# A four-layer graph network on one core: score banks seeded by VectorE, bias banks by ScalarE, and ScalarE's tile operand left in its own bank

## The chip, the core and the metric

The kernel runs on one NeuronCore of a Trainium2 chip. Four engines compute: TensorE (PE, matmuls, writes only PSUM), VectorE (DVE), ScalarE (ACT) and GpSimd (POOL, which works on SBUF alone here); SyncE (SP) issues transfers. PSUM has eight banks of 128 partitions x 512 fp32 values. The metric is device microseconds of one execution; lower is better. Three runs of the kernel before gave 4797.05 to 4799.08 us, median 4798.81.

## What is computed

Input `x` has 64 batches of 256 nodes with 128 features; `adj` is 256 x 256. Four layers, each on a layer norm with ReLU of what the layer before gave, and each added to its input:

```
layer 0: 5 gated steps   m = adj @ h; z, r = sigmoid(...); hv = tanh(...); h = (1-z)*h + z*hv
layer 1: relu([h, adj^T h, (2 adj^T adj^T - 1) h, ...] @ Theta1 + bias)
layer 2: y = (adj @ h + h) @ weight + bias;  y / max(|y|, 1e-12)
layer 3: e[i,j] = sum_f a[f] * leaky(s1[i,f] + s2[j,f] + b_lin[f]) + adj[i,j]
         out = sigmoid(softmax_j(e) @ h)
```

Layer 3 is most of the work: for each batch 256 x 256 node pairs times 256 features f, with a nonlinear step for each, so nothing but the sum over f can be a matmul.

## The kernel before

Batches are taken in 32 pairs. A **front** (`front`, L485) does layers 0 to 2 and layer 3's projections for one pair, as a chain of some 109 steps; the first pair is done as two single batches (`alone`), whose code paths differ a little. All tensors of a step are 128 x 512 (features x 2 batches x 256 nodes, or nodes x features), one bank.

Layer 3 is done in **slots**, 64 for a pair, 32 for each of its two **units**. A unit covers 128 rows i for both batches of the pair. A slot treats 4 rows x 2 batches; it needs two **tiles** of 128 x 2048, one for each half k of the 256 features. A tile holds min(s2, row of s1) or the ReLU that stands for it. Any of three engines can make a tile (`work_on_tile`, L908):

- VectorE, k = 0: one TENSOR_TENSOR (L928) that reads `s1a` in SBUF and `s2a` in the bank where TensorE wrote it.
- ScalarE, k = 1: 8 ACTIVATEs of 128 x 256 (L940), which read a bank and take a column of `s1b` as bias.
- GpSimd, k = 0 or 1: 8 TENSOR_SCALARs of 128 x 256 (L945) on copies in SBUF, `s2c` and `s2n`.

The operand that ScalarE reads comes about in three moves: TensorE projects it into a bank, ScalarE copies it to SBUF (`s2n`, L763), the bank is given back, and at the first ScalarE tile of a pair ScalarE copies `s2n` into one bank kept for this alone all along (`S2P`, L935).

`score` (L989) sums a tile over features: four matmuls side by side, each against a window of a column of signs, into the unit's **score bank**. A unit's first score begins the bank: TensorE multiplies the adjacency by an identity into it (8 matmuls of 128 x 256, through `side_by_side`, L403), and every score accumulates on that. For 600 of the 2048 slots the two tiles are added first by a DMA that GpSimd issues (L965), so one score serves for both. In all 3496 scores.

When a unit's 64 tiles are in, its **tail** (`tail`, L803) follows: VectorE adds `lin` (a row vector that a DMA has spread over the partitions, `rows`, L753) to the bank (L809), adds the part of one odd feature (L814), takes the maximum (L819); ScalarE exponentiates; TensorE transposes and multiplies; then the division, tanh and output.

In layers 1 and 2 of a front, `project_token` (L436) multiplies into a bank `po`, and VectorE adds the bias there, bank to bank (L664, L687), before it goes on (L668; L691 on ScalarE).

**The order** of every engine's instructions is fixed when the program is built, by a planner in the kernel (from L1032 on). It keeps a clock per engine with a cost for each step (`ran`, L107; a tile 2.2 on VectorE, 2 x 1.43 on ScalarE, 4 x 0.9 on GpSimd; a score 0.86). On the engine whose clock is lowest it takes, of the steps that are ready, a tail's first, then a front's, then a score, then a new tile. A result is seen by others `SEEN` later (0.18 us for ScalarE), and for ScalarE a further `behind` later, which grows by 0.024 of its work and shrinks by its gaps:

```python
        if engine == ACT:
            behind[0] = max(0.0, behind[0] - (start - clock[ACT])) + 0.024 * us
        clock[engine] = start + us
        return clock[engine] + SEEN[engine] + (behind[0] if engine == ACT else 0.0)
```

Fronts are held to due times by the number of scores done, and may not run more than two steps ahead. Tiles have 14 buffers, banks are in a list `spare` with the time when each comes free (`take`, L121, gives the earliest), and at most two score banks are open. Each engine then runs its fixed list in order, and waits at each instruction for what it needs.

Of the kernel before, what the change touches and what calls it, by code (L numbers as in the profile page):

```python
# [9 lines left out]
AF = mybir.ActivationFunctionType  # L10
# [4 lines left out]
P = 128  # L15
# [17 lines left out]
def kernel(  # L33
# [70 lines left out]
    SEEN = {PE: 0.25, DVE: 0.14, ACT: 0.18, POOL: 0.13}  # L104
    behind = [0.0]

    def ran(engine, us, *after):  # L107
        start = max(clock[engine], 0.0, *after)
        if engine == ACT:
            behind[0] = max(0.0, behind[0] - (start - clock[ACT])) + 0.024 * us  # L110
        clock[engine] = start + us
        return clock[engine] + SEEN[engine] + (behind[0] if engine == ACT else 0.0)

# [6 lines left out]

    def take():  # L121

        spare.sort(key=lambda b: b[1])
        return spare.pop(0)

# [282 lines left out]
    def project(pp, w, t, start=True, stop=True):  # L408

        side_by_side(pp[:, 0:t.shape[1] * N], w, flat(t), start, stop)  # L410

    def mix_nodes(pm, h, a):

        nb = h.shape[1]
        pm = by_feature(pm, nb)
        for b in range(nb):
            for c in range(NC):
                side_by_side(pm[:, b, :], h[:, b, c, :], a[:, c, :], c == 0, c == NC - 1)

# [15 lines left out]

    def project_token(pp, pairs):  # L436

        nb = pairs[0][0].shape[1]
        pp = by_token(pp, nb)
        for b in range(nb):  # L440
            for c in range(NC):
                for k, (t, w) in enumerate(pairs):
                    side_by_side(pp[:, b, c, :], t[:, b, c * P:(c + 1) * P], w, k == 0, k == len(pairs) - 1)

# [36 lines left out]
    READY = {}  # L481
    S2P = []
    OF_FIRST = {}

    def front(p, batches):  # L485
# [164 lines left out]
        yield ACT, t  # L650
        hT, t = copied("hT", b, t, bufs=4)
        yield PE, t_h, 1
        b = take()
# [3 lines left out]
        c2T, t = copied("c2T", b, t)  # L657
        yield PE, t, 1
        po = take()
        project_token(po[0], [(hT, th[:, 0, :]), (c1T, th[:, 1, :]), (c2T, th[:, 2, :])])  # L660
        t = ran(PE, PRODUCTS[nb], t, po[1])
        yield DVE, t
        pt = rows_of(turned_of(po))
        nc.vector.tensor_add(pt, pt, bias1.unsqueeze(1).to_broadcast([P, nb * NC, D]))  # L664
        t = ran(DVE, ELEMENTS[nb], t)
        yield DVE, t
        x2 = token("x2", tag="x12", bufs=3)
# [5 lines left out]
        h = token("h")  # L673
        t = yield from norm(x2, t, h)
        yield PE, t, 1
        b = take()
# [3 lines left out]
        yT, t = copied("yT", b, t)  # L680
        yield PE, t, 1
        po = take()
        project_token(po[0], [(yT, w2)])
        t = ran(PE, PRODUCT[nb], t, po[1])
        yield DVE, t
        pt = rows_of(turned_of(po))
        nc.vector.tensor_add(pt, pt, bias2.unsqueeze(1).to_broadcast([P, nb * NC, D]))  # L687
        t = ran(DVE, ELEMENTS[nb], t)
        yield ACT, t
# [67 lines left out]
        yield PE, t_hT, 1  # L757
        b = take()
        project(b[0], w2n[:, P:2 * P], hT)
        t = ran(PE, PROJECT[nb], t_hT, b[1])  # L760
        yield ACT, t
        s2n = kept("s2n", [N])
        nc.scalar.copy(s2n, seen(b))  # L763
        t_2 = ran(ACT, COPY[nb], t)
        spare.append([b[0], t_2])
        s2p = []
        if alone:
            yield ACT, t_2, not S2P
            if not S2P:
                S2P.append(take())  # L770
            s2p.append(by_feature(S2P[0][0])[:, own])
            nc.scalar.copy(s2p[0], s2n)
            ran(ACT, COPY[nb], t_2, S2P[0][1])
        yield PE, t_hT, 1
# [16 lines left out]
        spare.append([b[0], t_n])  # L791
        ops = dict(x3=x3, h3=h3, s1=(s1a, s1b), s2a=seen(s2a), bank=s2a, s2c=s2c, s2n=s2n, s1o=s1o, s2o=s2o, s2p=s2p,
                   lin=lin, t_lin=t_lin, since=(max(t_n, t_s2a), max(t_b, t_2), max(t_b, t_2)), alone=alone,
                   left=SLOTS // 2 if alone else SLOTS)
        for u in batches:
            READY[p, u] = ops
        tiles.extend([t, max(t_b, t_n, t_lin)] for t, _ in lent)

# [4 lines left out]
    def tail(u, pe, since):  # L803

        ops = READY[u]
        x3, h3, pe, lin = ops["x3"], ops["h3"], [by_feature(pe[0])[:, k, :] for k in range(NB)], ops["lin"]
        yield DVE, max(since, ops["t_lin"])
        used = banks_of.pop(u)
        nc.vector.tensor_add(by_feature(used), by_feature(used), lin.to_broadcast([P, NB, N]) if ops["alone"] else lin)  # L809
        t = ran(DVE, ELEMENTS[2], since, ops["t_lin"])  # L810
        yield DVE, t
        sc = feat("sc", **SHORT)
        for k, (b, c) in enumerate(across(u)):
            nc.vector.scalar_tensor_tensor(sc[:, k, :], ops["s2o"][:, b, :], ops["s1o"][:, b, c:c + 1], pe[k], op0=OP.min, op1=OP.add)  # L814
        t = ran(DVE, 0.8, t)
        spare.append([used, t])
# [91 lines left out]
    def work_on_tile(e):  # L908
        if e not in begun:
            k = part_of(e)  # L910
            tiles.sort(key=lambda t: t[1])
            begun[e] = [slot(k), k, *tiles.pop(0), 0]
            following[k] += 1
            held[e] += 1
            if k == 0:
                READY[where(begun[e][0])[0]]["left"] -= 1
        n, k, t, free, part = begun[e]
# [8 lines left out]
        if e == DVE:  # L926
            whole = [P, 4, NB, N]
            nc.vector.tensor_tensor(t, rows.to_broadcast(whole), ops["s2a"].unsqueeze(1).to_broadcast(whole), op=OP.min)  # L928
            done = ran(DVE, 2.2, since)
            ops["bank"][1] = max(ops["bank"][1], done)  # L930
            parts = 1
        elif e == ACT:
            if not ops["s2p"]:
                ops["s2p"].append(by_feature(S2P[0][0]))
                nc.scalar.copy(ops["s2p"][0], ops["s2n"])  # L935
                ran(ACT, 0.62, since)
            parts = 2
            for g in (2 * part, 2 * part + 1):
                for b in range(NB):
                    nc.scalar.activation(t[:, g, b, :], other(ops["s2p"][0], b), AF.Relu, bias=rows[:, g, b], scale=-1.0)  # L940
            done = ran(ACT, 1.43, since)
        else:
            parts = 4
            for b in range(NB):
                nc.gpsimd.tensor_scalar(t[:, part, b, :], other(ops["s2n" if k else "s2c"], b), rows[:, part, b],  # L945
                                        MOST_NEGATIVE, op0=OP.min, op1=OP.max)
            done = ran(POOL, 0.9, since)
        begun[e][4] += 1
        if part + 1 == parts:
# [3 lines left out]
            else:  # L953
                made.append((done, n, k, t, e))
        if k == 0 and not ops["left"] and ops["bank"][0] is not None:
            spare.append(list(ops["bank"]))
            ops["bank"][0] = None

# [4 lines left out]
    def add_pair(n):  # L963
# [7 lines left out]
        made.append((done, n, 2, t, None))  # L971

    def score_ready():

        best = None
        for tile_ in made:
            u, _ = where(tile_[1])
            since = tile_[0]
            if u not in left:
                if len(banks_of) == 2 or not spare:  # L980
                    continue
                since = max(since, min(b[1] for b in spare))
            if best is None or since < best[0]:
                best = since, tile_
        return best
# [3 lines left out]
    def score(tile_):  # L989
        since, n, k, t, e = tile_  # L990
        u, r = where(n)
        made.remove(tile_)
        if u not in left:
            left[u] = 64
            bank, free = take()
            banks_of[u] = bank
            for x, (_, c) in enumerate(across(u)):
                side_by_side(by_feature(bank)[:, x, :], ident, adj_n[:, c, :], x == 0, False)
            ran(PE, 0.87, since, free)
        left[u] -= 2 if k == 2 else 1  # L1000
        pe = banks_of[u]
        w = win if e == ACT else win_n
# [29 lines left out]
    def chain_ready(key, e):  # L1032

        engine, since, bank, gate = (*CHAINS[key][1], 0, None)[:4] if len(CHAINS[key][1]) < 4 else CHAINS[key][1]
        if engine != e or bank and not spare or gate and not gate():
            return None
        if not isinstance(key, tuple) and 1 <= key < NPAIR and spare:

            due = STEPS_OF_FRONT * (scored[0] / (2 * SLOTS) - (key - 2)) / SPREAD
            if CHAINS[key][2] > due + AHEAD:  # L1040
                return None
        return max(since, min(b[1] for b in spare)) if bank else since

# [14 lines left out]
    while scored[0] < 2 * NSLOT or CHAINS:  # L1058
# [12 lines left out]
        else:  # L1071
            since = tile_ready(e)
            if since is not None:
                todo.append((since, (3,), None))
            pair = pair_ready()
            if e == POOL and pair and e not in begun:
                todo.append((pair[0] + SLACK, (2,), pair[1]))
        ready = [x for x in todo if x[0] <= now[e] + 0.05]
        if ready:
# [5 lines left out]
            elif e == PE:  # L1085
                score(what)
            elif rank == 2:
                add_pair(what)
# [38 lines left out]
```

## Time and profile before

| | us |
|---|---|
| median of three runs | 4798.81 |
| the profiled execution | 4796.37 |
| its span | 4794.6 |
| TensorE busy, matmuls | 4744.3 |
| VectorE, ScalarE, GpSimd busy | 4651.6, 4608.6, 4636.5 |
| VectorE tiles, L928, x1747 | 3909.3 |
| ScalarE tiles, L940, x9976 | 3937.4 |
| GpSimd tiles, L945, x6408 and x2408 | 3056.0, 1167.1 |
| scores, L1004, x27968 (two matmul records each) | 2241.6 and 1317.3 |

A line of the groups reads: source line, engine, operation, what it writes and reads, shapes and count; then the busy time of the group, the mean duration of one, and how long its engine had been idle before it. A duration on ScalarE or VectorE includes the landing of its result, which overlaps with the next instruction: 9976 activations of 704 ns on average would be 7023 us, and their busy time is 3937. So the time that an instruction takes from a full engine is read from the distance of two starts. The clock granted to TensorE was 0.999 of full speed. The first 148 us are set-up and the first pair's front, in which VectorE, ScalarE and GpSimd are not yet full; from 4540 us on no fronts are left.

### The profile page before, as it was taken

What the parts mean: (1) busy time and instruction counts of PE and PEld (TensorE: products, weight loads), DVE (VectorE), ACT (ScalarE), POOL (GpSimd) and SP (SyncE); (2) the same over time, 40 slices, a digit from 0 to 9 for tenths busy, and PEclk for the clock granted to TensorE, in tenths of its full rate; (3) what the DMA queues carried; (4) which work ended last, traced back from release to release, by engine and by line L of the source; (5) the groups of instructions that cost most, each with busy time, mean ns of one, the idle gap of its engine ahead of it and who ended that gap; (6) DMA issues with size and microseconds to landing.
All of it is one profiled execution on the core that took longest, in us unless ns stands there. A gap on an engine that the chain in (4) does not pass through costs nothing.

```text
span 4794.6 us, 134766 instructions
## 1 busy us (share of the span) xinstructions
PE 4744.3 (99%) x52583; PEld 1758.2 (37%) x52583; DVE 4651.6 (97%) x3568; ACT 4608.6 (96%) x12063; POOL 4636.5 (97%) x9919
## 2 busy tenths in 40 slices
PE   9999999999999999999999999999999999999999
PEld 4333333433333333333333333333333333333333
DVE  6999999999999999999999999999999999999999
ACT  6999999999999999999999999999999999999999
POOL 3999999999999999999999999999999999999998
PEclk9999999999999999999999999999999999999999
DMA  1767777777676777777777777777767777777730
GB/s 39 151 142 154 150 146 150 145 145 158 141 157 143 143 155 152 151 146 145 149 152 149 147 150 146 151 155 146 148 138 158 150 151 151 148 150 143 151 66 5
DMA packets 131529, 672.82 MB, mean 140 GB/s; under 512 B 14920, under 2 KB 50120, under 8 KB 54088
## 3 DMA queue, kind: packets, MB, share of 16 engines
q0 software_dynamic: 86400, 629.18, 65.6%
q1 hardware_dynamic: 43768, 35.01, 2.5%
q8 instruction: 411, 6.73, 0.6%
q14 instruction: 230, 1.88, 0.1%
q10 hardware_dynamic: 720, 0.00, 0.0%
HBM read 26.48 MB, written 8.52 MB: 7 GB/s over the span
## 4 chain that ended last, share of the span: by engine, by line
PE 69%; DVE 10%; POOL 8%; DMA 6%; ACT 5%; issue 2%; POOLq 0%; SPq 0%; DVEq 0%; ACTq 0%
PE bank L1004 43%; PE bank L403 23%; DVE rl L928 8%; POOL rl L945 7%; DMA rl<-rl 5%; ACT rl L940 3%; PE bank L434 2%; PE bank L426 1%; POOL rl L965 1%; ACT h L478 0%; DVE bank L613 0%; DVE d L609 0%; DVE hT L617 0%; DVE rh L574 0%; POOL mv L398 0%
## 5 line engine op out<-in xcount | busy, mean ns | idle before, releaser
L940 ACT ACTIVATE rl<-bank,s1b 128x256 f32<-128x256 f32 x9976 | 3937.4, 704 | 47.5 <-DMA rl<-rl 18.7
L928 DVE TENSOR_TENSOR rl<-s1a,bank 128x2048 f32<-128x2048 f32 x1747 | 3909.3, 2276 | 41.4 <-DMA rl<-rl 19.5
L945 POOL TENSOR_SCALAR rl<-s2n,s1b 128x256 f32<-128x256 f32 x6408 | 3056.0, 799 | 19.5 <-ACT s1b L780 5.1
L1004 PE MATMUL bank<-rl,win_n 128*32 128x512 f32 x17992 | 2241.6, 593 | 20.8 <-DMA rl<-rl 14.9
L1004 PE MATMUL bank<-rl,win 128*32 128x512 f32 x9976 | 1317.3, 593 | 0.0
L945 POOL TENSOR_SCALAR rl<-s2c,s1a 128x256 f32<-128x256 f32 x2408 | 1167.1, 763 | 3.5
L1004 PEld LDWEIGHTS bank<-rl,win_n 128*32 128x32 f32 x17992 | 577.4, 110 | 1197.8 <-issue 978.2
L965 POOL DMA_DIRECT2D rl<-rl x600 | 644.9, 1090 | 3.6 <-PE bank L1004 0.9
L1004 PEld LDWEIGHTS bank<-rl,win 128*32 128x32 f32 x9976 | 324.8, 110 | 636.4 <-issue 516.5
L403 PE MATMUL bank<-mT,wts 128*32 128x512 f32 x2480 | 328.1, 592 | 0.5 <-ACT mT L526 0.5
L403 PE MATMUL bank<-adj_t,h 128*32 128x256 f32 x4960 | 296.8, 379 | 3.8 <-ACT h L628 3.8
L403 PEld LDWEIGHTS bank<-adj_t,h 128*32 128x32 f32 x4960 | 160.0, 110 | 160.8 <-issue 49.6
L478 ACT ACTIVATE h<-x,mv 128x128 f32<-128x128 f32 x376 | 163.8, 584 | 26.8 <-POOL mv L474 26.5
L403 PE MATMUL bank<-mT,w 128*32 128x512 f32 x1240 | 165.3, 593 | 0.6 <-ACT bank L570 0.5
L570 ACT ACTIVATE bank<-bank,gate_b 128x512 f32<-128x512 f32 (+1 forms) x165 | 137.6, 834 | 29.4 <-PE bank L403 16.5
L403 PE MATMUL bank<-rh,u5t 128*32 128x512 f32 x1240 | 164.9, 592 | 0.0
L403 PE MATMUL bank<-hT,wts 128*32 128x512 f32 x1240 | 163.5, 593 | 0.0
L403 PEld LDWEIGHTS bank<-mT,wts 128*32 128x32 f32 x2480 | 82.3, 110 | 185.1 <-issue 149.4
L398 POOL TENSOR_TENSOR mv<-mv,minus_half 128x4 f32<-128x4 f32 (+1 forms) x132 | 133.8, 1014 | 11.0
L593 ACT ACTIVATE bank<-bank,gate_b 128x512 f32<-128x512 f32 (+1 forms) x165 | 134.6, 816 | 10.2 <-PE bank L403 10.1
L526 ACT COPY mT<-bank 128x512 f32<-128x512 f32 x155 | 123.8, 799 | 19.6 <-PE bank L403 19.6
L606 ACT ACTIVATE bank<-bank,gate_b 128x512 f32<-128x512 f32 x155 | 128.8, 831 | 6.3 <-PE bank L403 6.3
(206 smaller groups left out, 3274.2 us busy)
## 6 DMA issues: line engine op xcount, KB each, us to landing
rl<-rl POOLq DMA_DIRECT2D x600, 1024.0 KB, 8.3
rows<-row SPq DMA_DIRECT2D x31, 512.0 KB
xin<-in_x_dram SPq DMA_DIRECT2D x64, 128.0 KB
out_dram<-o SPq DMA_DIRECT2D x64, 128.0 KB
row<-quarter SPq DMA_DIRECT2D x62, 2.0 KB
rows<-row SPq DMA_DIRECT2D x2, 256.0 KB
w_raw<-in_L_gnn_w_w_dram SPq DMA_DIRECT2D x3, 128.0 KB
rl<-in_L_gnn_Theta_dram SPq DMA_DIRECT2D x1, 320.0 KB
```

The lines of the kernel that those rows point to most:

```text
L398: nc.gpsimd.tensor_tensor(t, t, minus_half[:, 0:t.shape[1]], op=OP.pow)
L403: nc.tensor.matmul(o[g:g + 32], w[:, g:g + 32], t, start=start, stop=stop, skip_group_check=True)
L478: nc.scalar.activation(h[:, k, :], s[:, k, :], AF.Relu, bias=mv[:, k, 0:1], scale=mv[:, k, 1:2])
L526: nc.scalar.copy(c, seen(bank))
L570: nc.scalar.activation(seen(r), seen(pr), AF.Tanh, bias=br, scale=0.5)
L593: nc.scalar.activation(seen(pr), seen(pr), AF.Tanh, bias=bz, scale=0.5)
L606: nc.scalar.activation(seen(pv), seen(pv), AF.Tanh, bias=bh_n, scale=-1.0)
L928: nc.vector.tensor_tensor(t, rows.to_broadcast(whole), ops["s2a"].unsqueeze(1).to_broadcast(whole), op=OP.min)
L940: nc.scalar.activation(t[:, g, b, :], other(ops["s2p"][0], b), AF.Relu, bias=rows[:, g, b], scale=-1.0)
L945: nc.gpsimd.tensor_scalar(t[:, part, b, :], other(ops["s2n" if k else "s2c"], b), rows[:, part, b], MOST_NEGATIVE, op0=OP.min, op1=OP.max)
L965: nc.gpsimd.dma_start(out=t.rearrange("p g b n -> p (g b n)"), in_=z.rearrange("p g b n -> p (g b n)"), accum_op=OP.add)
L1004: nc.tensor.matmul(pe[g * 32:(g + 1) * 32, :], w[:, 31 - r:63 - r], flat(t[:, g]), start=False, stop=(left[u] == 0), skip_group_check=True)
```

## The change

- **Score banks.** For all units but the first pair's two, VectorE writes the sum of the adjacency and `lin` into the score bank ahead of the unit's first score (`fill_bank`, L1006 of the changed file), when the pair's operands are ready and one engine's next tile lies in that unit. TensorE's copy through the identity goes, and so does VectorE's addition of `lin` in the tail. The scores accumulate on what VectorE wrote.
- **Biases.** ScalarE copies the bias into the bank `po` ahead of the product, and the product accumulates on it; VectorE's additions (L664, L687) go. The bank is taken one mixing step earlier.
- **Which banks.** [...] a set `WRITTEN` keeps account of banks that matmuls have wholly written, and only those may be filled by VectorE or ScalarE (`take(2)`). `mix_nodes` and `project_token` start fresh once per bank instead of once per piece, so that the whole bank stays marked.
- **ScalarE's operand.** It reads the bank into which TensorE projected it. That bank is given back when the pair's last ScalarE tile has begun. The private bank and its 31 copies (and 2 halves) go.
- **The planner** loses `behind`: a ScalarE result is seen 0.18 us after its step in every case. `take` prefers, of the banks that are free by now, those not in `WRITTEN`.

```diff
-    behind = [0.0]
     def ran(engine, us, *after):
         start = max(clock[engine], 0.0, *after)
-        if engine == ACT:
-            behind[0] = max(0.0, behind[0] - (start - clock[ACT])) + 0.024 * us
         clock[engine] = start + us
-        return clock[engine] + SEEN[engine] + (behind[0] if engine == ACT else 0.0)
+        return clock[engine] + SEEN[engine]
...
+    WRITTEN = set()
+    def of_spare(bank):
+        return [b for b in spare if bank < 2 or id(b[0]) in WRITTEN]
-    def take():
-        spare.sort(key=lambda b: b[1])
-        return spare.pop(0)
+    def take(bank=1):
+        b = min(of_spare(bank), key=lambda b: (max(b[1], min(now.values())), bank < 2 and id(b[0]) in WRITTEN, b[1]))
+        spare.remove(b)
+        if bank < 2:
+            WRITTEN.discard(id(b[0]))
+        return b
...
+        if not alone:
+            yield ACT, t, 2
+            po = take(2)
+            nc.scalar.copy(rows_of(turned_of(po)), bias1.unsqueeze(1).to_broadcast([P, nb * NC, D]))
+            t_po = ran(ACT, COPY[nb], po[1])
         yield PE, t_h, 1
         b = take()
         mix_nodes(b[0], h, adj_2)
...
-        project_token(po[0], [(hT, th[:, 0, :]), (c1T, th[:, 1, :]), (c2T, th[:, 2, :])])
+        project_token(po[0], [(hT, th[:, 0, :]), (c1T, th[:, 1, :]), (c2T, th[:, 2, :])], fresh=alone)
...
-        nc.vector.tensor_add(pt, pt, bias1.unsqueeze(1).to_broadcast([P, nb * NC, D]))
+        if alone:
+            nc.vector.tensor_add(pt, pt, bias1.unsqueeze(1).to_broadcast([P, nb * NC, D]))
...
-        nc.vector.tensor_add(by_feature(used), by_feature(used), lin.to_broadcast([P, NB, N]) if ops["alone"] else lin)
+        if ops["alone"]:
+            nc.vector.tensor_add(by_feature(used), by_feature(used), ops["lin"].to_broadcast([P, NB, N]))
...
-            if not ops["s2p"]:
-                ops["s2p"].append(by_feature(S2P[0][0]))
-                nc.scalar.copy(ops["s2p"][0], ops["s2n"])
-                ran(ACT, 0.62, since)
-                    nc.scalar.activation(t[:, g, b, :], other(ops["s2p"][0], b), AF.Relu, bias=rows[:, g, b], scale=-1.0)
+                    nc.scalar.activation(t[:, g, b, :], other(ops["s2b"], b), AF.Relu, bias=rows[:, g, b], scale=-1.0)
...
+    def bank_ready():
+        u = next((u for u in UNITS if u not in left and u not in banks_of), None)
+        if u not in READY or READY[u]["alone"] or len(banks_of) == 2 or all(where(slot(k))[0] < u for k in range(3)):
+            return None
+        return (max(READY[u]["t_lin"], min(b[1] for b in of_spare(2))), u) if of_spare(2) else None
+    def fill_bank(u):
+        bank, free = take(2)
+        nc.vector.tensor_add(by_feature(bank), adj_n[:, u[1]:u[1] + 1, :].to_broadcast([P, NB, N]), READY[u]["lin"])
+        banks_of[u] = bank, ran(DVE, ELEMENTS[2], free, READY[u]["t_lin"])
```

Layer 2's bias is treated as layer 1's is. On VectorE the fill stands in the planner's choice after tails' and fronts' steps and ahead of new tiles.

## The prediction

> **What bounds the kernel now.** I read the page's busy shares first, then the table by stage, the chain, the groups of the lines that change, and stretches of each engine's timeline. The page's opening lines:
>
> ```profile
> span 4794.6 us, 134766 instructions
> PE 4744.3 (99%) x52583; PEld 1758.2 (37%) x52583; DVE 4651.6 (97%) x3568; ACT 4608.6 (96%) x12063; POOL 4636.5 (97%) x9919
> ...
> PE 69%; DVE 10%; POOL 8%; DMA 6%; ACT 5%; issue 2%; POOLq 0%; SPq 0%; DVEq 0%; ACTq 0%
> ```
>
> All four engines are nearly full; the last line, the chain that ended last, is on TensorE for 69% of its length, so no other engine can be called the bound alone. By stage, the part without start and end (148 to 4540 us):
>
> ```profile
> core 0: us, PE busy (x) PEld busy (x) DVE busy (x) ACT busy (x) POOL busy (x), PEclk, DMA share, GB/s
> ...
> 2100.00:2800.00 700.00, 696.29 (x7644) 251.62 (x7640) 687.82 (x515) 679.94 (x1782) 690.49 (x1473) 1.00 0.73 148
> ...
> sum 4392.00, PE 4364.79 PEld 1605.74 DVE 4309.21 ACT 4263.65 POOL 4336.88; mean PE 623.54 PEld 229.39 DVE 615.60 ACT 609.09 POOL 619.55
> ```
>
> Idle in those 4392 us: TensorE 27, VectorE 83, ScalarE 128, GpSimd 55. ScalarE alone has room worth naming. A tile goes to whichever engine the planner finds free, so an engine's share of tiles follows from its other work.
>
> Busy times of groups overlap; what an engine gives per instruction when full is read from starts in its timeline:
>
> ```profile
> 1327.96 6.36 ACT L940 ACTIVATE rl<-bank,s1b 128x256 f32<-128x256 f32 x16
> 1333.67 1.13 ACT L526 COPY mT<-bank 128x512 f32<-128x512 f32 x1
> ```
>
> 16 activations in 1333.67 − 1327.96 = 5.71 us: 0.357 each, 2.86 per tile of 8.
>
> ```profile
> 831.43 0.59 ACT L935 COPY bank<-s2n 128x512 f32<-128x512 f32 x1
> 832.06 3.03 ACT L940 ACTIVATE rl<-bank,s1b 128x256 f32<-128x256 f32 x8
> ```
>
> A ScalarE copy from SBUF into a bank: 0.63.
>
> ```profile
> 1119.00 0.69 DVE L613 SCALAR_TENSOR_TENSOR bank<-bank,d 128x512 f32<-128x512 f32 x1
> 1119.60 2.27 DVE L928 TENSOR_TENSOR rl<-s1a,bank 128x2048 f32<-128x2048 f32 x1
> 1121.80 0.68 DVE L617 SCALAR_TENSOR_TENSOR hT<-bank,hT 128x512 f32<-128x512 f32 x1
> ```
>
> VectorE: 0.60 for 512 columns, 2.20 for a tile.
>
> ```profile
> 835.94 1.05 PE L403 MATMUL bank<-adj_n,ident 128*32 128x256 f32 x16
> 836.80 1.04 PE L1004 MATMUL bank<-rl,win 128*32 128x512 f32 x8
> ```
>
> TensorE: 0.86 for one unit's copy of the adjacency. In the chain, 24 GpSimd instructions of L945 take 10.92 us: 0.455 each, 3.64 per tile of 8.
>
> **The change, part by part.** Counts are from the instruction orders of the two built programs.
>
> TensorE. 62 of 64 adjacency copies go: 62 × 0.86 = −53 us. No matmul is added: the bias steps only turn a fresh start into accumulation. Scores stay 3496.
>
> VectorE. 62 adds of biases (L664, L687, 0.69 a row, 0.60 in sequence) go: −37. The 62 adds of `lin` in the tails go and 62 fills with the adjacency plus `lin` come: alike in size, taken at nothing. VectorE also gets 4 tiles fewer (1747 to 1743): −9. Sum −46.
>
> The fill is the one operation with no row of its kind: both inputs lie in SBUF, while L809, which it replaces, and the tiles (L928) read one from PSUM. By the row (L633 reads SBUF and a bank in 0.68, L809 in 0.69) it costs its 0.60 and nobody else anything. The Trainium skill speaks against it (SBUF — State Buffer, "Who interferes with whom"): a VectorE instruction with two SBUF inputs takes its second through the read port that GpSimd uses, and whichever of the two starts second stands until the first is done. GpSimd reads SBUF all the time (0.455 per instruction). By the rule GpSimd stands up to 62 × 0.60 = 37 us and VectorE, arriving mid-instruction, 62 × 0.23 = 14. No row here shows it. Bounds: 0 and 37 + 14; a gain is excluded, since the columns are the same. I take it as it says, about 37 and 14 of engine time.
>
> ScalarE. 31 copies into the private bank (0.63) go, −20; 62 bias copies come at the same row, +39 (bounds 0.47, the PSUM-to-SBUF copy at 1333.67 to 1334.14, and 0.63: +29 to +39). Tiles go from 1247 to 1264: 17 × 2.86 = +49. Sum +68, against 128 us idle.
>
> GpSimd. Tiles 1102 to 1089: 13 × 3.64 = −47. The 600 adding DMAs stay, as do SP's issues; no queue gets a transfer more.
>
> Banks. The private bank is freed, but each pair keeps a second bank until its last ScalarE tile has begun, so where two pairs meet four banks are held (three before); a score bank is filled some 4 VectorE tiles ahead, and a bias bank is taken before the mixing matmuls instead of after. Only banks that matmuls have wholly written may serve. The price is a front held up for want of a bank. In the order, the operands of a pair stand about 7.5 ScalarE tiles before their first use, before and after alike, so I take nothing; the bound is one bank's turnover, about 1 us in each of 31 pairs, hidden under 7.5 × 2.86 = 21 us of lead.
>
> New waits. The fill waits for the DMA of `rows`; queued behind it are VectorE's tiles. It stands about 11 tiles (24 us) behind the transpose that starts those rows, and in the trace the rows are issued 4 us after that transpose: nothing. The product with theta waits for ScalarE's bias copy, which is issued ahead of a mixing step (1.7 us of matmuls) and an evacuation: hidden, about 0.6 us per use on a front that is early anyway. What this cover hides costs 62 × 0.6 = 37 us of front, not of span.
>
> The planner's lag term. `behind` goes: in the plan a ScalarE result is now visible 0.18 us after its slot always. The rows show why the term was there: an L940 lasts 449 ns at least, 659 in the median, 704 on average, 1930 at most, so results land 0.255 us later on average than a fresh one, more after long runs without a gap. ScalarE's gaps shrink from 128 to about 60, so runs get longer. The LDWEIGHTS waits put down to an L940 are 603 (79.6, 83.5, 25.6 and 14.3 us by line), 0.34 each, where the ordinary spacing is 0.29: the handoff is just in time. If a third of these are late by 0.25, TensorE loses 50; VectorE takes about 400 ScalarE results in its fronts and loses perhaps 10. Bounds: below nothing is excluded, since an optimistic plan makes nothing land sooner; above, 603 × 0.255 = 154.
>
> **The sum.** In engine time: TensorE −53 + 50 = −3; VectorE −46 + 14 + 10 = −22; GpSimd −47 + 37 = −10; ScalarE +68 into its gaps. Without lag and port it would be −53, −46, −47. TensorE's late starts do not add to the lock, and the 14 tile buffers let an engine catch up, so I put the losses on the span at half of what they cost the engine: −46 (VectorE and GpSimd agree) + about 12 for the port (half of 14 and 37 averaged) + about 10 to 15 for the lag = −22 to −24. The profiled execution took 4796.4 (span 4794.6 and 1.8 around it), 2.4 under the median of the runs, 4798.8. So 4798.8 − 24 = 4775.
>
> **The rivals.**
> A. Nothing lost: port and lag cost nothing and the plan's relief comes through. 4799 − 46 = 4753. For it: three engines get the same relief. Against: two of the costs have reasons. With forecast and A in one family, chance of the forecast's case (4753 to 4789) 0.45, of A or better 0.08.
> B. No gain: only the engines that make tiles bind. Then TensorE's 53 us are cover. VectorE's 37 us are worth 37 / 2.2 = 17 tiles, ScalarE's 19 extra cost 7, GpSimd's 37 of blocking cost 10: zero tiles, 4799. For it: GpSimd hardly waits (8 us in the steady part). Against: the orders give VectorE and GpSimd 46 and 47 us less work, so the plan has found the time. 0.16.
> C. Slower: ScalarE's late results. Place: the first LDWEIGHTS behind an L940 or a front's evacuation. If all 603 just-in-time handoffs stand by half the lag, 603 × 0.13 = 78: 4799 − 46 + 78 = 4831. It decides from 46 / 603 = 0.076 us per handoff on. For it: the term was cut while ScalarE is given 68 us more. Against: PE's own idle is 27 us in all, and most waits fall into its queue's spacing. 0.31.
> D. The change not doing what it says: a fill that isn't accumulated on; the bookkeeping of written banks answers that, and it would move no time.
>
> **How the numbers follow.** 4775 is the likeliest case. A measurement of this kernel tells about 0.2% from no change, so faster is below 4789.2 and slower above 4808.4: 0.53, 0.16, 0.31. The likeliest case alone reaches from 4753 to 4789; for 8 in 10 the range goes from 4745 (A with a little of ScalarE's gaps) into C, to 4824.
>
> **What would show it.** L403 from adj_n and ident x16 in place of x1024; the fill's row at 0.69, or above 0.8 if it waits for the port; L945's mean (799 and 763) and the gaps of GpSimd around a fill; L940's mean above 704; LDWEIGHTS waits on L940 above 203 us in all; ScalarE at 98%, VectorE and GpSimd no fuller than now. I am wrong if TensorE's steady idle stays at 27 us while ScalarE's share does not rise, or if a wait for a bank comes to the top of the waits.

## The result, and the profile after

The changed kernel takes 4810.46 us (median of 11 runs, 4798.15 to 4824.08); the kernel before, run in turn with it, 4798.35 (11 runs, 4795.99 to 4799.47). The ratio is 1.0028, 95% interval 1.002 to 1.0035: slower by 0.28%, where a gain of 0.5% was forecast. Its own runs spread over 26 us, those of before over 3.5. The profiled execution took 4805.16. Beside e5 to e8 the kernel before took 4810.1 us instead of some 4798, so the experiments below are compared by their ratios to it and not by their times (against 4798 those four would stand at 1.001, 1.003, 0.995 and 1.010, and no conclusion turns on that). The page, opening lines and the chain that ended last:

```profile
span 4803.4 us, 132787 instructions
...
PE 4724.4 (98%) x51591; PEld 1748.8 (36%) x51591; DVE 4660.5 (97%) x3502; ACT 4661.5 (97%) x12228; POOL 4616.3 (96%) x9815
...
PE 58%; ACT 16%; DVE 11%; POOL 9%; issue 4%; DMA 3%; POOLq 0%; DVEq 0%; ACTq 0%
```

TensorE and GpSimd did get less to do (20 us less busy each), and ScalarE more (53). VectorE, which was to get 46 us less, is 9 us busier. The chain runs over TensorE for 58% instead of 69%, and over ScalarE for 16% instead of 5%. The steady stretch in the table by stage (columns as before):

```profile
148.00:4540.00 4392.00, 4327.86 (x47380) 1581.65 (x47372) 4312.73 (x3162) 4306.87 (x11292) 4310.66 (x9137) 1.00 0.73 149
```

Idle there: TensorE 64 us (27 before), VectorE 79 (83), ScalarE 85 (128), GpSimd 81 (55). The relief came back as TensorE and GpSimd standing still, with VectorE as busy as ever. The groups say with what:

```profile
L961 ACT ACTIVATE rl<-bank,s1b 128x256 f32<-128x256 f32 x10112 | 4085.3, 850 | 12.1 <-DMA rl<-rl 9.1 <-POOL rl L967 1.2 <-PE bank L1041 0.7
...
L1006 DVE TENSOR_TENSOR bank<-adj_n,rows 128x512 f32<-128x512 f32 x62 | 97.1, 1566 | 0.0
```

The fill takes 1566 ns on average where the forecast's two cases were 690 and "above 800". The view of that one line gives minimum, median and maximum in ns:

```profile
L1006 DVE TENSOR_TENSOR bank<-adj_n,rows x62: 684/880/6761, 233.4 to 4669.6; 128x512 f32<-128x512 f32 x62
```

The mean hides two kinds. 47 fills end within 1.3 us; 15 take 58.5 us together, the longest 6.76. Above 690 ns each, the 62 lose 54 us: the 47 short ones 6, the 15 long ones 48. Here is the longest, in VectorE's timeline (start, us, what):

```profile
1553.79 6.76 DVE L1006 TENSOR_TENSOR bank<-adj_n,rows 128x512 f32<-128x512 f32 x1
1560.47 0.68 DVE L622 TENSOR_TENSOR d<-bank,hT 128x512 f32<-128x512 f32 x1
...
1566.06 0.68 DVE L630 SCALAR_TENSOR_TENSOR hT<-bank,hT 128x512 f32<-128x512 f32 x1
```

GpSimd meanwhile, with what ended its idle time in brackets:

```profile
1552.65 4.29 POOL L967 TENSOR_SCALAR rl<-s2n,s1b 128x256 f32<-128x256 f32 x8
1556.23 4.63 POOL L967 TENSOR_SCALAR rl<-s2c,s1a 128x256 f32<-128x256 f32 x8
1563.97 0.88 POOL L987 DMA_DIRECT2D rl<-rl  x1 [3.11 <-DVE bank L626]
```

Eight starts in 1556.23 − 1552.65 = 3.58 us are 0.448 each, GpSimd's undisturbed pace. It hardly notices the fill, which stands beside 14 of its instructions and ends only when these have run out. Then GpSimd itself idles for 3.11 us, since its next step, the issue of an adding DMA, waits for VectorE. Before such issues it idles 25.7 us in all, 14 of them put down to VectorE, against 3.6 in the kernel before:

```profile
L987 POOL DMA_DIRECT2D rl<-rl x600 | 649.6, 1099 | 25.7 <-DVE rl L953 9.7
```

```profile
L965 POOL DMA_DIRECT2D rl<-rl x600 | 644.9, 1090 | 3.6 <-PE bank L1004 0.9
```

Four of the long fills end like this one, when GpSimd has run out. The others, and the short ones, get in between two of its instructions: the short ones behind three at most, the long ones behind as many as 15. At a fill that gets in beside the making of tiles, a start of GpSimd comes some 1 us after the one before instead of 0.448: 39 of the spacings in this trace lie between 0.8 and 1.1 us, and none in e1, e3 and e7 below. Over all fills GpSimd lost about 19 us that way, 0.3 for each, and VectorE 54. Why some fills are let in at once and others are not, the trace does not show. What follows is seen on TensorE:

```profile
1560.73 1.04 PE L1041 MATMUL bank<-rl,win_n 128*32 128x512 f32 x8
1566.79 1.11 PE L447 MATMUL bank<-ident,hT 128*128 128x128 f32 x4 [5.01 <-DVE hT L630]
```

A front's `hT` is late by the fill; TensorE stands in its fixed order for 5.01 us, and in about these 5 us ScalarE is busy for only 3.43 and GpSimd for 2.03 (the first row of the table further down). TensorE's waits for that `hT` (us in total, times, longest), after and then before:

```profile
PE bank L447 <- DVE hT L630: 32.8, 15, 5.7
```

```profile
PE bank L434 <- DVE hT L617: 5.8, 15, 0.7
```

TensorE also comes back slower. The table by stage around that stand (TensorE's clock is the third number from the right):

```profile
1561.00:1566.00 5.00, 0.78 (x8) 0.00 (x0) 5.00 (x4) 3.43 (x10) 2.03 (x5) 0.87 0.13 28
1566.00:1569.00 3.00, 2.21 (x12) 1.11 (x16) 3.00 (x4) 1.06 (x3) 2.42 (x6) 0.50 1.08 218
1569.00:1573.00 4.00, 4.00 (x36) 1.19 (x32) 4.00 (x2) 2.45 (x7) 3.54 (x8) 0.69 0.98 197
```

A mean of 0.87 over 5 us is half clock for the last 1.3 of them: the clock fell about 3 us into the stand. TensorE works again from 1566.79 on, at half clock until about 1571.5 (0.69 over the last 4 us is half clock for 2.5 of them). The Trainium skill (TensorE: Matmul & The Clock Gate, Part 1) has this: half rate after an idle window of about 3.4 us, full rate after a busy one. The lengths in the trace agree: six drops in this execution, each 3.4 or 6.8 us long, 30.7 us in all, and none in the kernel before between its start-up and its end. The idle time before them agrees only roughly: the six begin 2.4 to 4.3 us into TensorE's six longest stands (3.6 to 5.7 us), and in e4 below three stands of 2.2 to 2.7 us brought drops as well.

### The profile page after: what moved, and what is told of

It reads as the page before. It is cut to its first block, busy times and chain, and to the rows that moved or that the text cites. A ratio compares the mean times of both kernels' runs of the same rounds, so it can differ in the third digit from the quotient of the medians.

```text
span 4803.4 us, 132787 instructions
## 1 busy us (share of the span) xinstructions
PE 4724.4 (98%) x51591; PEld 1748.8 (36%) x51591; DVE 4660.5 (97%) x3502; ACT 4661.5 (97%) x12228; POOL 4616.3 (96%) x9815
## 4 chain that ended last, share of the span: by engine, by line
PE 58%; ACT 16%; DVE 11%; POOL 9%; issue 4%; DMA 3%; POOLq 0%; DVEq 0%; ACTq 0%
PE bank L1041 37%; PE bank L414 18%; ACT rl L961 12%; DVE rl L953 8%; POOL rl L967 7%; DMA rl<-rl 3%; PE bank L447 2%; ACT h L492 1%; POOL rl L987 1%; POOL mv L409 1%; PE bank L439 1%; ACT bank L619 0%; DVE bank L1006 0%; DVE hT L630 0%; DVE bank L626 0%
## 5 line engine op out<-in xcount | busy, mean ns | idle before, releaser
L961 ACT ACTIVATE rl<-bank,s1b 128x256 f32<-128x256 f32 x10112 | 4085.3, 850 | 12.1 <-DMA rl<-rl 9.1
L1041 PE MATMUL bank<-rl,win 128*32 128x512 f32 x10112 | 1358.1, 595 | 0.0
L967 POOL TENSOR_SCALAR rl<-s2c,s1a 128x256 f32<-128x256 f32 x2440 | 1189.7, 779 | 3.4
L1041 PEld LDWEIGHTS bank<-rl,win_n 128*32 128x32 f32 x17856 | 588.5, 110 | 1170.8 <-issue 971.6
L987 POOL DMA_DIRECT2D rl<-rl x600 | 649.6, 1099 | 25.7 <-DVE rl L953 9.7
L1041 PEld LDWEIGHTS bank<-rl,win 128*32 128x32 f32 x10112 | 336.7, 110 | 672.2 <-issue 515.0
L583 ACT ACTIVATE bank<-bank,gate_b 128x512 f32<-128x512 f32 (+1 forms) x165 | 161.5, 979 | 18.6 <-PE bank L414 14.4
L606 ACT ACTIVATE bank<-bank,gate_b 128x512 f32<-128x512 f32 (+1 forms) x165 | 159.1, 964 | 7.6 <-PE bank L414 7.6
L539 ACT COPY mT<-bank 128x512 f32<-128x512 f32 x155 | 146.5, 945 | 15.5 <-PE bank L414 15.5
L619 ACT ACTIVATE bank<-bank,gate_b 128x512 f32<-128x512 f32 x155 | 152.9, 986 | 2.4 <-PE bank L414 2.4
```

The costliest lines, as they stand in the source:

```text
L539: nc.scalar.copy(c, seen(bank))
L583: nc.scalar.activation(seen(r), seen(pr), AF.Tanh, bias=br, scale=0.5)
L606: nc.scalar.activation(seen(pr), seen(pr), AF.Tanh, bias=bz, scale=0.5)
L619: nc.scalar.activation(seen(pv), seen(pv), AF.Tanh, bias=bh_n, scale=-1.0)
L961: nc.scalar.activation(t[:, g, b, :], other(ops["s2b"], b), AF.Relu, bias=rows[:, g, b], scale=-1.0)
L987: nc.gpsimd.dma_start(out=t.rearrange("p g b n -> p (g b n)"), in_=z.rearrange("p g b n -> p (g b n)"), accum_op=OP.add)
```

## The experiments

Ratios are to the kernel before, run in turn on the same chip, with 95% intervals. The theory after the result was that the fill's second SBUF input costs the whole loss, and the rivals were the cut lag term and the banks.

### The port

**e1_one_input.** The fill copies the adjacency alone, one input; `lin` is left out of the output. Every engine's order is that of the changed kernel.

```diff
-        nc.vector.tensor_add(by_feature(bank), adj_n[:, u[1]:u[1] + 1, :].to_broadcast([P, NB, N]), READY[u]["lin"])
+        nc.vector.tensor_copy(by_feature(bank), adj_n[:, u[1]:u[1] + 1, :].to_broadcast([P, NB, N]))
```

> The changed kernel, except that the fill copies the adjacency alone into the score bank (one input in SBUF in place of two); lin is left out of the scores, so that part of the computation is missing. Every engine's order is that of the changed kernel. Theory P (the fill stands for GpSimd's read port): the fill's mean falls from 1566 ns to about 690, VectorE gets 54 us back, TensorE's long stands behind VectorE's hT go, its granted clock is 0.999 again, and the runs agree within some 5 us: 4755 to 4780. Theory L (ScalarE's late results, which the plan no longer counts): the fill was only where the lateness showed; 4800 to 4812.

Measured: 0.9909 (0.9894 to 0.9924), 4750.08 us. Its groups (of its slowest execution, 4770.66):

```profile
L961 ACT ACTIVATE rl<-bank,s1b 128x256 f32<-128x256 f32 x10112 | 4112.3, 876 | 14.3 <-DMA rl<-rl 11.7 <-POOL rl L967 1.2 <-issue 0.5
...
L1006 DVE COPY bank<-adj_n 128x512 f32<-128x512 f32 x62 | 42.4, 684 | 0.0
```

With one input a fill takes 684 ns. Same orders, 1.19% apart: 57 us. ScalarE's results are later here than in the changed kernel (876 against 850), so their lateness is not what cost the time. It is theory P; the gain is larger than its range, which began at 4755.

**e7_two_steps.** `lin` comes back, as a second VectorE instruction that reads the bank and one SBUF input: the kernel's whole output, and 62 instructions more than the changed kernel has.

```diff
+        nc.vector.tensor_copy(by_feature(bank), adj_n[:, u[1]:u[1] + 1, :].to_broadcast([P, NB, N]))
+        nc.vector.tensor_add(by_feature(bank), by_feature(bank), READY[u]["lin"])
```

> The changed kernel with the fill in two VectorE instructions, a copy of the adjacency and then an add of lin in the bank, each with one input in SBUF; the plan counts both. Theory P: fills of 0.69 us each, no stands, clock 0.999; VectorE carries 37 us more, so 4760 to 4780.

Measured: 0.9927 (0.9912 to 0.9941).

```profile
L1007 DVE TENSOR_TENSOR bank<-bank,rows 128x512 f32<-128x512 f32 x62 | 43.3, 699 | 2.1
L1006 DVE COPY bank<-adj_n 128x512 f32<-128x512 f32 x62 | 42.3, 683 | 0.0
```

Two instructions, 85.6 us busy, beat the one at 97.1, and not one of the 124 stood (689 and 700 ns at most), as theory P has it. So neither `lin` nor its transfer is the cost, but the two SBUF inputs of one instruction.

**e3_scalar_fill.** ScalarE copies the adjacency into the bank, VectorE adds `lin` in the tail as before.

```diff
+        nc.scalar.copy(by_feature(bank), adj_n[:, u[1]:u[1] + 1, :].to_broadcast([P, NB, N]))
+        banks_of[u] = bank, ran(ACT, COPY[2], free)
```

> The changed kernel, except that ScalarE copies the adjacency into the score bank (62 copies of about 0.52 us, 32 us more for ScalarE) and VectorE adds lin in the tail as before; no VectorE instruction has two inputs in SBUF. Theory P: clock 0.999, small spread, 4765 to 4785. Theory L: ScalarE is fuller still, 4812 or more.

Measured: 0.9919 (0.9905 to 0.9933), 4755.97 us, a full version that beats both kernels. Theory P again, and again below its range.

**e4_double_fill.** The changed kernel's fill, issued twice in a row.

> The changed kernel with each fill done twice in a row by VectorE; the plan does not know of the second, so all orders are the same otherwise. Theory P: 62 more adds that each may stand for the port: between 0.6 and 1.5 us each, 37 to 97 us on VectorE, 4840 to 4890, clock 0.993 or lower. Theory L: 62 x 0.6 = 37 us on VectorE, most of it on the span, 4830 to 4845, clock as in the changed kernel.

Measured: 1.0117 (1.0101 to 1.0132).

```profile
L1006 DVE TENSOR_TENSOR bank<-adj_n,rows 128x512 f32<-128x512 f32 x62 | 118.3, 1909 | 0.0
...
L1007 DVE TENSOR_TENSOR bank<-adj_n,rows 128x512 f32<-128x512 f32 x62 | 58.0, 936 | 2.1
```

This is theory P. The second fill, right behind the first, waits far less: 849 ns in the median, though once 7.8 us. The two stand 91 us beyond 690 ns each, and 37 us of work (62 x 0.60) are added; the time is 2.1% (100 us) above e1.

**e12_fill_in_pieces.** Each fill as four additions of 128 columns, again with two SBUF inputs, to let GpSimd in between.

```diff
+        for x in range(NB):
+            for c in range(NC):
+                nc.vector.tensor_add(by_feature(bank)[:, x, c * P:(c + 1) * P], adj_n[:, u[1], c * P:(c + 1) * P], READY[u]["lin"][:, x, c * P:(c + 1) * P])
```

> The changed kernel with the fill cut into four adds of 128 columns, each with two inputs in SBUF; all orders as in the changed kernel. If each instruction has to win the port anew, the four of a fill take more than 2.5 us together, and the ratio is above 1.010. If a short one slips in more easily, or the four run on once the port is won, 1.5 us or less and 0.998 to 1.004.

Measured: 1.0073 (1.0058 to 1.0088).

```profile
L1008 DVE TENSOR_TENSOR bank<-adj_n,rows x248: 290/449/8997, 232.1 to 4703.5; 128x128 f32<-128x128 f32 x124
```

Four times as many starts, 98 us beyond the shortest piece's 290 ns, and 1.64% (79 us) above e1. The four of a fill take 2.7 us together, as in the first case, but the ratio stays under that case's 1.010, and they do not each stand alike: the first takes 1.48 us on average and up to 9.0, each of the other three 0.41 to 0.43. As in e4, an addition that follows at once is soon let in. Over the three kernels the loss on the span was 57 us for 54 of standing, 79 for 98, and in e4 100 for 91 and 37 of work: some eight tenths of it or more.

### TensorE's relief

**e6_tensor_fill.** All of the change but the fill: TensorE writes the adjacency through the identity, `lin` is added in the tail.

> The changed kernel, except that TensorE writes the adjacency into the score bank through the identity as before and VectorE adds lin in the tail; biases and ScalarE's operand as in the change, no behind. TensorE has its 53 us again, VectorE and ScalarE are as in the change. Theory R: half or more of the 48 us is lost, 4775 to 4800. Theory G: 4750 to 4765.

Measured: 1.0008 (0.9999 to 1.0016). All of the gain is lost, the far end of theory R. Against e3 the difference is 0.9%: what e3 wins hangs on TensorE's 53 us, and the rest of the change wins nothing measurable while TensorE keeps these copies.

**e11_bias_on_vector.** e3 with the biases of layers 1 and 2 added by VectorE as before.

> ScalarE's fill, but the biases added by VectorE as before (62 adds of 0.60, 37 us) and no bias copies on ScalarE (62 of 0.51, 32 us). The plan shifts tiles (VectorE 1731, ScalarE 1273, GpSimd 1092). If moving the biases matters by itself: 0.996 to 1.000. If only TensorE's relief counts, since tiles go where there is room: 0.991 to 0.994.

Measured: 0.9935 (0.992 to 0.9949). Moving the biases is worth 0.16% by these two ratios, which their intervals don't resolve; the case in which only TensorE's relief counts.

### The planner's lag term

**e2_lag_back.** The changed kernel with `behind` put back.

```diff
+            behind[0] = max(0.0, behind[0] - (start - clock[ACT])) + 0.024 * us
...
+        return clock[engine] + SEEN[engine] + (behind[0] if engine == ACT else 0.0)
```

> The changed kernel with the planner's behind put back. The plan gives ScalarE 22 tiles fewer (1242), VectorE 18 more, GpSimd 4 more. Theory P: the fill's mean stays above 1300 ns, granted clock below 0.999, spread of 10 us or more, 4795 to 4810. Theory L: 4750 to 4775, with ScalarE's activations back at about 700 ns on average, and a small spread.

Measured: 1.0178 (1.0163 to 1.0192), 1.5% above the changed kernel. The cut of the term, for which the forecast charged 10 to 15 us, had gained 72. Neither theory foresaw this: the time lies above both ranges, the fill's mean fell to 1242 ns, and the activations are at 748.

**e5_before_no_lag.** The kernel before without `behind`.

> The kernel before, with the planner's behind taken out and nothing else (plan: ScalarE 1258 tiles in place of 1247, VectorE 1738, GpSimd 1100). Theory R (the relief of TensorE, VectorE and GpSimd is what the one-input fill's 48 us come from): the term is worth little by itself, 4790 to 4810. Theory G (the gain is the term's removal, the rest only moves work): 4750 to 4775. Theory L of the prediction (without the term, results are late): 4810 to 4830.

Measured: 0.9988 (0.9981 to 0.9995): there the term is worth 0.1%, as theory R has it.

**e8_scalar_fill_lag.** e3 with `behind`, to have it without the port.

> ScalarE's fill with the planner's behind put back. If the 77 us that the term added to the changed kernel came from the fill's stands falling on a tighter plan: 4750 to 4765, as without the term. If the term itself spoils the plan of this structure (operands of a pair late, GpSimd waiting for s1b): 4810 to 4850, and waits of GpSimd for s1b of more than 20 us in all.

Measured: 1.0081 (1.0066 to 1.0097), 1.6% above e3: the second case, the term itself spoils the plan. The waits that stand out:

```profile
PE bank L1043 <- DMA rl<-rl: 60.5, 63, 3.5
...
POOL rl L969 <- ACT s1b L804: 28.2, 4, 10.1
```

GpSimd waits at four starts of a pair for a front's `s1b` (once, 4.9 us, in e3). In ScalarE's instruction order `s1b` is written some 7.6 tiles ahead of its first use in e3; in e8 three pairs have no such lead. So the next theory was that `behind` makes fronts late.

**e9_lag_early_fronts** and **e10_early_fronts.** e8 and e3 with fronts due earlier.

```diff
-    STEPS_OF_FRONT, SPREAD, AHEAD = 109, 1.8, 2
+    STEPS_OF_FRONT, SPREAD, AHEAD = 109, 1.4, 2
```

> ScalarE's fill with the planner's behind, and fronts due earlier (SPREAD 1.4 in place of 1.8): in the instruction order nearly every pair's operands now stand 5 to 20 ScalarE tiles ahead of their first use. If the 1.6% that the term cost this structure came from fronts that end too late, it is back near the kernel with ScalarE's fill, ratio 0.990 to 0.997. If it comes from elsewhere (the plan holds ScalarE's results back and gives it fewer tiles, 1224), 1.003 to 1.010.

> The control to the earlier fronts: the same without behind. Fronts were in time already, so earlier ones should be worth nothing or cost some banks: ratio 0.990 to 0.998.

Measured: e9 1.0106 (1.0089 to 1.0123), e10 0.9994 (0.9986 to 1.0003), both just above their ranges (for e9, that of its second case). Earlier fronts cost 0.75% by themselves, and between the two the term still costs 1.1%. Late fronts may be a part; as the cause the theory falls.

What was left is the form of the term: it grows by 0.024 of all work and shrinks only in gaps, so over a long stretch the plan either leaves ScalarE 2.4% of gaps or takes its results for ever later. The steady stretch of e3 and then e8:

```profile
148.00:4540.00 4392.00, 4354.28 (x47671) 1589.79 (x47664) 4294.78 (x3187) 4359.76 (x11399) 4342.07 (x9212) 1.00 0.73 150
```

```profile
148.00:4540.00 4392.00, 4301.22 (x47084) 1569.73 (x47080) 4267.53 (x3160) 4250.05 (x11069) 4298.85 (x9140) 1.00 0.72 148
```

ScalarE idles 32 us (0.7%) without the term and 142 (3.2%) with it.

**e13_lag_capped.** e8 with the term held to 0.4 us.

```diff
+            behind[0] = min(0.4, max(0.0, behind[0] - (start - clock[ACT])) + 0.024 * us)
```

> The kernel of e8 (ScalarE's fill, behind put back), but behind held to at most 0.4 us. Uncapped it grows by 0.024 us per us of work and shrinks only in gaps, so over a long stretch the plan has to leave ScalarE 2.4% of gaps or hold back whoever waits for its results. Theory P (the unbounded growth is what costs; a bounded lag of the size that the trace shows costs nothing): 0.990 to 0.995 of the kernel before, as e3 at 0.992, ScalarE idle in the steady part at 30 to 60 us of 4392. Theory Q (any lag put into the plan costs, since a plan with later results has less to choose from): 1.000 to 1.008, as e8.

Measured: 0.992 (0.9905 to 0.9935), theory P. Its steady stretch:

```profile
148.00:4540.00 4392.00, 4356.56 (x47892) 1592.69 (x47885) 4308.43 (x3194) 4366.90 (x11422) 4337.22 (x9246) 1.00 0.74 150
```

ScalarE idles 25 us, just under what theory P expected; its results are later than in any other run here:

```profile
L963 ACT ACTIVATE rl<-bank,s1b 128x256 f32<-128x256 f32 x10056 | 4145.4, 939 | 3.4 <-DMA rl<-rl 1.9 <-PE bank L1043 0.8 <-POOL rl L969 0.3
```

**e14_lag_slow_growth.** e8 with 0.008 in place of 0.024.

> The kernel of e8 with behind growing by 0.008 us per us of work in place of 0.024, uncapped. Theory P (the forced gaps are what costs): a third of e8's distance to e3 (1.6%), so 0.994 to 0.999 of the kernel before; ScalarE idle in the steady part near 60 to 80 us, between e3's 38 and e8's 142 as the page counts it. Theory Q (any lag costs): 1.003 to 1.008.

Measured: 0.9955 (0.994 to 0.997), ScalarE's steady idle 54 us: between e3 (32, not the 38 named above) and e8, as a cost by growth would have it. The term costs 0.36% here against 1.6% in e8, which is rather less than a third.

**e15_tensor_fill_lag.** e6 with `behind`.

> The kernel of e6 (the change with TensorE's own fill through the identity kept and lin added in the tail: 1.001 of the kernel before) with behind put back. Theory P: behind costs where TensorE leaves ScalarE no gaps of its own accord; here, as in the kernel before, TensorE's 53 us are still on the path and ScalarE has gaps anyway, so behind costs at most 0.3%: 0.999 to 1.004. Theory R (behind costs through ScalarE's bias copies and its longer share of the front, which before lacks): 1.010 to 1.018, as behind cost 1.5% in e2 against the change.

Measured: 1.0003 (0.9995 to 1.0012) against e6's 1.0008, theory P. The steady stretch of e6 and then e15:

```profile
148.00:4540.00 4392.00, 4350.74 (x48248) 1589.53 (x48240) 4272.53 (x3166) 4268.43 (x11144) 4318.74 (x9185) 1.00 0.73 148
```

```profile
148.00:4540.00 4392.00, 4356.45 (x48413) 1599.22 (x48406) 4298.92 (x3183) 4247.47 (x11102) 4328.92 (x9238) 1.00 0.73 149
```

ScalarE idles 124 us without the term and 145 with it. Where TensorE still makes its copies, ScalarE has gaps anyway and the term costs nothing; with TensorE relieved (e3 and e8), it takes the place of 32 us of gaps with 142. That the term costs through its growth and not as a lag of up to 0.4 us is shown by e13 and e14. That the gaps of ScalarE are what carries the cost to the span is argued from these idle times. On TensorE it appears as waits for the tiles of adding DMAs: 60.5 us in e8 against 19.4 in e3 and 19.1 in e13.

## Why the prediction was wrong

It failed in two terms of its sum. The port was put at about 12 us on the span and cost 57; that turned the gain into a loss. The cut of the lag term was put at 10 to 15 us of loss, while the gain would not have come without that cut. The second error is of the other sign but did not make up for the first, since the forecast had counted the relief in full already. With the sizes measured against e1, −44 for the relief and +57 for the port, the sum is the 13 us that were lost; this is no test of its own, since both come from e1.

- **The relief, −46.** Right in size: e1 is 44 us under before by its ratio (36 to 51), close to the 4753 of rival A. It hangs on TensorE's 53 us (e6) and hardly on VectorE's biases (e11), so that the sums of VectorE and GpSimd agreed on 46 was no proof of it. Wrong was to count it apart from the lag term's cut: e8, with TensorE relieved, no port cost and the term in place, is slower than before.
- **The port, 37 on GpSimd and 14 on VectorE, half on the span, about 12.** This step failed. Measured: about 19 and 54, and 57 on the span (e1 against the change, same orders). The split was the wrong way round. "VectorE, arriving mid-instruction, 62 × 0.23" took the Trainium skill's rule (SBUF — State Buffer, "Who interferes with whom": the second to start stands until the first is done) to mean one GpSimd instruction. For the 47 short fills that is near enough: they lost 0.13 us each, 6 in all. The other 15 stood beside several of GpSimd's instructions, up to 15, and lost 48. e7, e1 and e3, without such an addition, have no such wait. Halving was wrong too: the bound "0 and 37 + 14" excluded what happened, and a stand of VectorE reaches TensorE through a front's `hT`, in an order that is fixed.
- **The lag term, +10 to +15.** Wrong in sign. Its cut gains 1.5% in the changed kernel and 1.6% in e3's form of it, and 0.1% in the kernel before. The forecast's reason, 603 just-in-time handoffs, can be read: TensorE's and its loads' waits put down to ScalarE's tiles were 206 us (611 of them) before, 220 (654) after and 263 (780) in e2, with the term. Landing 0.15 to 0.24 us later (850 and 939 ns against 704) cost nothing that e13 could show.
- **ScalarE, +68 into its gaps.** About right: +53 busy, steady idle 128 to 85, and in e1 and e3, where others do not hold it up, to 45 and 32.
- **VectorE's −46** became +9, by the fill's 54. **GpSimd's −47** shows as 20 less busy and 26 more idle; before the adding DMAs it idles 22 more.
- **Banks and new waits, nothing.** Right: e1, with the same banks and orders, reaches the time of "nothing lost", and no wait for a bank is among TensorE's longest.
- **The rivals.** A was right but for the port. B took TensorE's 53 us for cover; e6 against e3 shows they are not. C had the sign, by the wrong mechanism; that the range reached up to 4824 and so took in the measured 4810 was C's doing, and luck. The signs that were named: fill above 0.8, yes; L940's mean above 704, yes (850), without harm; waits on it above those of before, yes, 220 against 206; ScalarE at 98%, not quite, 97. The adjacency copies that remain have 32 records, not the 16 written: two units, two records for each of 8 matmuls.

Open: why e8 is slower than before though its ScalarE idles little more (142 against 128 us). Its TensorE idles 91 us in the steady part against 27, much of it in waits for adding DMAs (60.5 against 14.9 over the span), but what makes these late was not followed. And that it is GpSimd's stream which holds the port is read from the traces and fits every run: the five fills that met none of GpSimd's tile instructions took 691 to 694 ns. No kernel was run with GpSimd stopped during a fill.

## What to carry to other kernels

Before moving work to VectorE beside a busy GpSimd, count its SBUF inputs: one instruction with two may have to stand beside many of GpSimd's, here up to 15 and in e4 more than 20, and two instructions with one each were faster (e7 against the change: 0.9927 and 1.0028). Don't judge a stand by its mean: of the 54 us here, 15 of the 62 fills made 48, so look at minimum, median and maximum of the line, and at who is next in the fixed order. Put a ceiling on a lag in a planner: here one that grew with all work cost 1.6% where one of at most 0.4 us cost nothing (e8 and e13 against e3).

## What the runs showed of the hardware

- A VectorE addition of 128 x 512 with both inputs in SBUF took 684 ns to 6.76 us beside GpSimd (10.4 us in e4, 9.0 us for a piece of 128 columns in e12); an immediate second one 936 ns on average against 1909 for the first. The same columns with one SBUF input took 673 to 691 ns as a copy (e1, e7) and 698 to 700 as an addition to a bank (e7).
- After a stand of 5 us TensorE's granted clock was at half for the next 3 us and more (0.50, then 0.69 over 4 us), so the stand cost more than its length. In e4 stands of 2.2 to 2.7 us brought such a drop, too.
- ScalarE's tile activations lasted 704 ns on average in the kernel before, with 2.9% of idle in the steady part, 866 in e3 with 0.7% and 939 in e13 with 0.6%. Fullness is not all of it: e8 has 805 with 3.2%. Longer records did not make a kernel slower: e3 and e13 have the same ratio, 0.992.
